# Summing a state scan's sixteen products on TensorE alone, instead of pairing them by accumulating DMAs first

## The chip, the cores and the metric

The kernel runs on one core of a Trainium2 chip. The metric is the device time of one execution in microseconds (us). Three executions of the kernel before took 10943.48, 10928.4 and 10927.6 us: the median is 10928.4 us.

## What is computed

The reference has two layers on a tensor `x` of 16 images, 128 channels, 64 x 64 pixels (4096 tokens an image). Cut to what matters here:

```python
# layer 0: a state space scan over the tokens of each image
xz = gn(x) @ W_in;  xs, z = split(xz)                 # 256 inner channels each
xc = silu(causal_conv(xs, conv_w) + conv_b)           # 4 taps
dt, Bm, Cm = split(xc @ W_xproj, [8, 8 + 16])
delta = softplus(dt @ W_dt + b_dt)
h_new = exp(delta * A) * h + (delta * xc)[:, :, None] * B_t   # 16 states n per channel
y = (h_new * C_t).sum(n) + xc * D
x = x + ((y * silu(z)) @ W_out)
# layer 1: attention with a running maximum and running sums over the tokens, 8 heads
k, v = silu(ln(t) @ W_kv);  s = q . k
m = cummax(s);  e = exp(s - m);  t = t + mean_over_heads(cumsum(e * v) / cumsum(e))
# then a gated feed-forward layer on 8 chosen tokens of each of 64 experts
```

The change is in the sum over `n` (the 16 states), and in the order of some steps of layer 1's attention that run in the same loop.

## The kernel before, in words

**The main loop** (line 710) runs over `k`: 128 blocks of 512 tokens (8 blocks an image), then 10 more rounds. Round `k` does three things at once: the scan of block `k` (`cur`), preparation of block `k + 1` (`nxt`: normalisation, convolution, projections), and the attention of a block nine behind (`m = k - 9`, and `mp_`, the one before it, whose second half is still open). So rounds 0 to 8 have scan alone, rounds 9 to 127 have all, and the last rounds have attention alone. After the loop come a routing stage, the experts, and the final sum (lines 922 to 1183).

**One round is 16 steps** `n`, one for each state (line 880). In step `n`, in this order: `product` (VectorE, `bx = du * B_n`), `beside(n)` (a list, written by hand, of work of the other blocks on TensorE and ScalarE, lines 734 to 878), `decays` (ScalarE, `da = exp(delta * A_n)` for up to eight states ahead), `load_bc` (SyncE's queue loads the rows B and C of three states ahead, broadcast to all partitions), `scan` (two VectorE scans of 128x512 with `between(n)` between them, then GpSimd's product `da <- h * C_n` into the tile of the decay), and `keep_state`. Every engine executes its own instructions in the order in which they are written down here; nothing is moved by a scheduler (`InOrder`, line 23, through which all of them go: hence the profile puts almost everything on L31, and tiles tell the operations apart).

**The sum over the states.** GpSimd leaves 16 tiles `da` of 128 x 2 x 512 a round. In steps 1, 3, ..., 13, `add_pair` (line 375, called at line 894) issues an accumulating DMA from GpSimd's queue that adds tile `n - 1` to tile `n`: 7 DMAs a round of 512 KB each. `add_y` (line 386) then adds one tile to the PSUM tile `y_ps`: 8 TensorE transposes of 128x128 in float32, each with its weight load. It is called for 9 tiles a round: the seven pair sums (at the ends of steps 4, 6, ..., 14 of the same round, line 899, and in step 0 of the next, line 745) and tiles 14 and 15 (step 1 of the next round), and once more for the term `xc * D` (step 2, which begins the sum). `take_y` (ScalarE, step 1), `turn_y` (8 transposes, step 2) and `gate` (VectorE, step 3, which needs TensorE's `yb_ps`) finish the previous block's y, `out_proj` projects it in step 5.

**What stands around it in the lists.** `weights` (two `w_ps` banks, filled by TensorE, read by ScalarE's exponential into `wm`), followed by `attend`, whose first matmuls `ao_ps` need `wm`. Step 7: `score_log`, the split of two numbers into three bf16 parts (`rest` on TensorE subtracts the part already taken, `split` on ScalarE rounds what is left), `conv(nxt, 1)` (the second product of the convolution: four taps, two passes each), `inverse` (four exponentials `e`), `finish`, and `store_parts` (a DMA from ScalarE's queue). `conv_silu` follows, behind a ScalarE table load. In step 10 `spread_parts` issues 16 small loads of those parts from SyncE's queue, and `load_bc` of later steps stands behind them in that queue. Short PSUM tiles of all kinds share 3 banks (`ps`), the tiles `da` have 13 buffers, the tiles B and C five. `from_chunks` (line 499) carries the running maximum and the running sum from one block to the next: line 510 copies two numbers a partition.

Of the kernel before, what the change touches and what calls it, by code (L numbers as in the profile page):

```python
# [39 lines left out]
def conv_attn_hybrid(ctx: ExitStack, tc: tile.TileContext, x, w_in, conv_w, conv_b, w_xproj, w_dt, b_dt,  # L40
# [40 lines left out]
    with ExitStack() as st:  # L81
# [201 lines left out]
            t = t[:, KC - 1 :] if w["i"] == 0 else t  # L283
            ACT.activation(t, t, AF.Identity, bias=gs[:, 4:5], scale=gs[:, 3:4])

        def conv(k, a):

            w = blocks[k]
            pt = w[f"xs{a}"] = bank("xs_ps")
            for t in range(KC):  # L290
                PE.matmul(pt, wc[:, t, bass.ts(a, P)], w["xb"][:, t : t + L], start=(t == 0), stop=(t == KC - 1))

        def conv_silu(k):
# [205 lines left out]
        def from_chunks(m, what, local, first, op0, op1, data):  # L499

            b, i = divmod(m, NBLK)
            last = stp.tile([P, 32], F32, tag=f"last_{what}", name=f"last_{what}")
            DVE.transpose(last, local[:, P - 32 :])
            z = zs[what][m % 2]
            if i == 0:
                DVE.memset(z[:, 0:10:5], first)
            else:
                DVE.tensor_copy(z[:, 0:10:5], gn[b][what][:, 4:14:5])  # L510
            gn[b][what] = z
            for g in range(2):
                DVE.tensor_tensor_scan(z[:, 5 * g + 1 : 5 * g + 5], bc(data[:, 0:1], [P, CB]),
                                       last[:, 5 * g : 5 * g + 4], z[:, 5 * g : 5 * g + 1], op0, op1)
            back = stp.tile([P, 32], F32, tag=f"back_{what}", name=f"back_{what}")
            DVE.transpose(back, z)
            return back[:, 31:32]
# [151 lines left out]


        LAG = NBLK + 1
        LEAD, LEAD_BC = 8, 3
        order = [(k, n) for k in range(NK) for n in range(N)]
        made = 0
# [35 lines left out]
        for k in range(NK + LAG + 1):  # L710
# [23 lines left out]
            def beside(n):  # L734

                if n == 0:
                    if mp_ is not None:
                        attend_before(mp_, 1)
                        add_x(mp_, 0)
                    if m is not None:  # L740
                        key(m, 0), key(m, 1), key(m, 2)
                    if mp_ is not None:
                        finish(mp_, 0)
                    if prev is not None:
                        add_y(prev, N - 3)
                if n == 1:
                    if m is not None:
                        key(m, 3), key(m, 4)
                        score(m, 0)
                    if prev is not None:  # L750
                        add_y(prev, N - 2)
                        add_y(prev, N - 1)
                    if nxt is not None:
                        norm_block(nxt)
                    if cur is not None:
                        skip(cur)
                    if prev is not None:
                        take_y(prev)
                if n == 2:
                    if m is not None:  # L760
                        key(m, 5), key(m, 6), key(m, 7)
                    if prev is not None:
                        turn_y(prev)
                    if cur is not None:
                        add_y(cur, -1)
                if n == 3:
                    if m is not None:
                        score(m, 1)
                    if prev is not None:
                        gate(prev)  # L770
                    if mp_ is not None:
                        for x in range(4, 8):
                            value(mp_, x // 2, x % 2)
                if n == 4:
                    load_exp()
                    if m is not None:
                        score_max(m)
                    if mp_ is not None:
                        weights(mp_, 2)
                    if ends is not None:  # L780
                        gn_end(ends, 1)
                if n == 5:
                    if mp_ is not None:
                        attend(mp_, 2)
                        weights(mp_, 3)
                    if m is not None:
                        score_exp(m)
                    if prev is not None:
                        out_proj(prev)
                    decays(k, n, 2)  # L790
                    if mp_ is not None:
                        carry_on(mp_, 2)
                if n == 6:
                    if mp_ is not None:
                        attend(mp_, 3)
                        attend_before(mp_, 2)
                    if nxt is not None:
                        conv(nxt, 0)
                    decays(k, n, 2)
                    if prev is not None:  # L800
                        put_back(prev)
                    if mp_ is not None:
                        carry_on(mp_, 3)
                    if ends is not None:
                        gn_end(ends, 3)
                if n == 7:
                    if mp_ is not None:
                        attend_before(mp_, 3)
                        add_x(mp_, 1)
                    if m is not None:  # L810
                        score_log(m)
                        rest(m, 1)
                    decays(k, n, 2)
                    if m is not None:
                        split(m, 1)
                    if nxt is not None:
                        conv(nxt, 1)
                    if m is not None:
                        rest(m, 2)
                        inverse(m)  # L820
                    if mp_ is not None:
                        finish(mp_, 1)
                    if m is not None:
                        split(m, 2)
                        store_parts(m)
                    if nxt is not None:
                        conv_silu(nxt)
                    if ends is not None:
                        gn_end(ends, 4)
                if n == 8:  # L830
                    if m is not None:
                        turn_weights(m)
                        value(m, 0, 0)
                    if nxt is not None:
                        xproj(nxt)
                        store_bc(nxt)
                    if m is not None:
                        value(m, 0, 1)
                if n == 9:
                    if mn is not None:  # L840
                        ln_center(mn)
                        ln_square(mn)
                    if cur is not None:
                        gate_silu(cur)
                    if k + 2 < NK:
                        load_block(k + 2, ACT)
                    if m is not None:
                        value(m, 1, 0), value(m, 1, 1)
                if n == 10:
                    if mn is not None:  # L850
                        ln_var(mn)
                    if nxt is not None:
                        delta(nxt)
                    load_exp()
                    if mn is not None:
                        ln_scale(mn)
                if n == 12:
                    if m is not None:
                        weights(m, 0)
                if n == 13:  # L860
                    if m is not None:
                        attend(m, 0)
                        attend_before(m, 0)
                        weights(m, 1)
                    decays(k, n, 2)
                    if m is not None:
                        carry_on(m, 0)
                if n == 14:
                    if mn is not None:
                        ln_apply(mn)  # L870
                    if m is not None:
                        attend(m, 1)
                    decays(k, n, 2)
                    if m is not None:
                        carry_on(m, 1)
                if n == 15:
                    if stat is not None:
                        gn_stats(*stat)

            for n in range(N):  # L880
                if cur is not None:
                    product(cur, n)
# [5 lines left out]
                if cur is not None:  # L888
# [2 lines left out]
                        load_bc(*order[later])  # L891
                    scan(cur, n, between)
                    keep_state(cur, n)
                    if n % 2 and n < N - 2:
                        add_pair(cur, n)
                else:
                    between(n)
                if cur is not None and n >= 4 and n % 2 == 0:
                    add_y(cur, n - 3)

                if 8 <= n <= 11 and i == 0 and prev is not None:
                    store_residual(b - 1, n - 8)
# [307 lines left out]
```

## Time and profile before

| What | Value |
|---|---|
| Median of three executions | 10928.4 us |
| The profiled execution | 10931.22 us |
| Its span, first to last instruction | 10929.5 us |
| Stretch 650 to 9430 us (rounds with scan and attention): busy TensorE, VectorE, ScalarE, GpSimd | 7915.26, 7760.89, 6248.85, 6827.48 us of 8780 |
| TensorE clock granted over the span | 0.890 |
| Tiles `da` added by DMA: issues, data, time of the packets | 896, 469.82 MB, 22.0% of 16 DMA engines |
| Transposes `y_ps<-ident,da` | 9216, 309 ns each as recorded |

The profile comes from one execution. "Busy" counts recorded instructions; TensorE's are pipelined and their ends are modelled, so starts are used below wherever possible. The clock is the share of full speed that the chip granted to TensorE. A wait is named by the instruction that ended it.

### The profile page before, as it was taken

The page shows a single profiled execution, that of the slowest core. Times are in us where ns is not written, and L with a number is a line of the kernel's source. Part 1 is how long each engine was busy: PE and PEld are TensorE (multiplying, and loading weights), DVE is VectorE, ACT ScalarE, POOL GpSimd, SP SyncE. Part 2 cuts the span into 40 slices and gives each one's busy share as a digit, 9 for nine tenths or more (in the row PEclk, how much of TensorE's full clock was granted, in tenths as well). Part 3 has the DMA queues.
Part 4 walks back from the last instruction along what each step waited for, and adds up shares of the span by engine and source line. Part 5 has one row for each costly group of instructions (what it writes and reads, how often), then busy time and mean ns, then how long its engine had stood idle before and what let it go on. Part 6 is the DMA issues. An engine that isn't in the chain of part 4 may idle for free.

```text
span 10929.5 us, 157776 instructions
## 1 busy us (share of the span) xinstructions
PE 9405.6 (86%) x55389; PEld 5549.3 (51%) x55389; DVE 9012.1 (82%) x9987; ACT 7284.5 (67%) x12924; POOL 7530.3 (69%) x4771
## 2 busy tenths in 40 slices
PE   4579998899988989998899999989899899888875
PEld 2345555555555555555555555555555555544752
DVE  8998888888888888888889888888888888820753
ACT  5567776777777777777777777777777777754640
POOL 7887777778777777777777777777777777820000
PEclk7789998999999999899998998999999899999886
DMA  7777767777677777776777777677777777721348
GB/s 191 199 205 182 198 178 199 181 193 184 179 199 181 195 179 195 185 195 181 187 190 184 194 181 200 176 199 180 193 187 176 198 178 192 184 65 34 109 154 343
DMA packets 944361, 1995.67 MB, mean 183 GB/s; under 512 B 103040, under 2 KB 188688, under 8 KB 936400
## 3 DMA queue, kind: packets, MB, share of 16 engines
q1 hardware_dynamic: 732912, 1414.88, 43.6%
q0 software_dynamic: 129024, 469.82, 22.0%
q10 hardware_dynamic: 81632, 100.88, 2.7%
q8 instruction: 439, 7.19, 0.3%
q14 instruction: 354, 2.90, 0.1%
HBM read 1363.98 MB, written 151.52 MB: 139 GB/s over the span
## 4 chain that ended last, share of the span: by engine, by line
PE 61%; ACT 18%; DVE 7%; DMA 7%; issue 5%; SPq 1%; ACTq 1%; POOL 1%; DVEq 0%; POOLq 0%
PE ao_ps L31 10%; PE k_ps L31 8%; PE v_ps L31 7%; PE xs_ps L31 7%; PE y_ps L31 6%; ACT da L31 5%; PE carry_ps L31 4%; PE o_ps L31 4%; DVE h L31 3%; PE s_ps L31 3%; ACT L219 3%; ACT wm L31 2%; PE dt_ps L31 2%; DVE bx L31 2%; PE dbl_ps L31 2%
## 5 line engine op out<-in xcount | busy, mean ns | idle before, releaser
L31 POOL TENSOR_TENSOR da<-h,bct 128x1024 f32<-128x1024 f32 x2048 | 6475.5, 3162 | 1943.1 <-DVE h L31 1521.5
L31 DVE TENSOR_TENSOR_SCAN h<-da,state,bx 128x512 f32<-128x512 f32 x3584 | 4414.6, 1265 | 169.5 <-DVE bx L31 3.4
L31 DVE TENSOR_TENSOR bx<-du,bct 128x1024 f32<-128x1024 f32 x2048 | 2598.3, 1269 | 470.3 <-DMA bct<-bcs 404.1
L31 ACT ACTIVATE da<-delta,a_neg 128x512 f32<-128x512 f32 x4096 | 2629.8, 716 | 89.5 <-DMA da<-da 61.4
L31 PE MATMUL y_ps<-ident,da 128*128 128x128 f32 x9216 | 1428.1, 309 | 279.2 <-DMA da<-da 278.9
L31 PEld LDWEIGHTS y_ps<-ident,da 128*128 128x128 f32 x9216 | 1210.5, 160 | 719.6 <-issue 401.8
L31 PE MATMUL ao_ps<-wm,v 128*128 128x128 f32 x8192 | 1266.4, 318 | 281.5 <-ACT wm L31 276.4
L31 PEld LDWEIGHTS ao_ps<-wm,v 128*128 128x128 f32 x8192 | 1182.1, 226 | 559.8 <-ACT wm L31 401.8
L31 PE MATMUL v_ps<-wv,xn 128*128 128x512 f32 x2048 | 1035.8, 629 | 257.0 <-ACT xc L31 240.9
L31 ACT ACTIVATE v<-v_ps 128x512 f32<-128x512 f32 x1024 | 606.3, 597 | 778.7 <-PE v_ps L31 669.1
L31 ACT ACTIVATE wm<-w_ps 128x512 f32<-128x512 f32 x1024 | 552.1, 590 | 608.7 <-PE w_ps L31 607.3
L31 PE MATMUL k_ps<-xn,wk 128*128 128x512 f32 x2048 | 944.4, 595 | 1.7 <-ACT kt L31 1.7
L31 PE MATMUL xs_ps<-xb,wc 128*128 128x512 f32 x2048 | 925.3, 595 | 1.8 <-issue 1.8
L31 POOL DMA_DIRECT2D da<-da x896 | 787.7, 879 | 163.9 <-POOL state L31 95.1
L31 PEld LDWEIGHTS v_ps<-wv,xn 128*128 128x128 f32 x2048 | 341.9, 192 | 787.5 <-issue 316.1
L31 ACT ACTIVATE kt<-k_ps 128x512 f32<-128x512 f32 x1024 | 587.3, 600 | 190.0 <-PE k_ps L31 166.2
L31 DVE TENSOR_TENSOR_SCAN h<-da,bx 128x512 f32<-128x512 f32 x512 | 599.8, 1206 | 25.5 <-ACT da L31 0.5
L31 PEld LDWEIGHTS xs_ps<-xb,wc 128*128 128x128 f32 x2048 | 372.0, 191 | 397.1 <-issue 382.5
L31 ACT ACT_TABLE_LOAD x395 | 506.8, 1283 | 51.6 <-ACT parts L31 45.9
L31 PEld LDWEIGHTS k_ps<-xn,wk 128*128 128x128 f32 x2048 | 371.6, 191 | 321.0 <-issue 254.7
L31 POOL COPY state<-h 128x2 f32<-128x2 f32 x1792 | 509.0, 284 | 0.0
L31 DVE TENSOR_TENSOR z<-yb_ps,z 128x512 f32<-128x512 f32 x256 | 164.8, 685 | 339.7 <-PE yb_ps L31 339.3
(196 smaller groups left out, 10931.1 us busy)
## 6 DMA issues: line engine op xcount, KB each, us to landing
bct<-bcs SPq DMA_DIRECT2D x2048, 512.0 KB
da<-da POOLq DMA_DIRECT2D x896, 512.0 KB, 8.1
xs<-t_d SPq DMA_DIRECT2D x240, 256.0 KB
xs<-in_x_dram SPq DMA_DIRECT2D x128, 256.0 KB
xt<-in_x_dram SPq DMA_DIRECT2D x64, 512.0 KB
t_d<-xt SPq DMA_DIRECT2D x64, 512.0 KB
t_d<-xs ACTq DMA_DIRECT2D x256, 128.0 KB
t<-t_d SPq DMA_DIRECT2D x128, 256.0 KB
```

What stands on the lines that cost most here:

```text
L31: return lambda *args, **kw: self.tc.keep_in_program_order(f(*args, **kw))
L219: tc.keep_in_program_order(nc.scalar.preload_act_table_set(EXP_LN))
```

## The change

Four edits, made together.

1. `PAIRS = ()`: no state is paired by a DMA any more; `add_pair` is never called. `add_y` is called for all 16 tiles: tile `n - 2` at the end of step `n` (2 to 15), tiles 14 and 15 in steps 0 and 1 of the next round. In step 8 the call stands ahead of `turn_weights` instead of at the end, so that tiles 5 (end of step 7) and 6 (start of step 8) follow one another.
2. The second product of the convolution is cut in two halves of two taps; `rest(m, 2)` stands between them on TensorE instead of behind all four taps.
3. On ScalarE in step 7: `finish(mp_, 1)` moves ahead of the first `split`, the two states of `decays` move from ahead of the first `split` to behind it, and `split(m, 2)` and `store_parts` move ahead of `inverse`.
4. Line 510's copy of two numbers becomes a `tensor_reduce` with a maximum over one element: the same numbers by another VectorE instruction.

```diff
-        def conv(k, a):
+        def conv(k, a, taps=range(KC)):
             w = blocks[k]
-            pt = w[f"xs{a}"] = bank("xs_ps")
-            for t in range(KC):
+            if taps[0] == 0:
+                w[f"xs{a}"] = bank("xs_ps")
+            pt = w[f"xs{a}"]
+            for t in taps:
                 PE.matmul(pt, wc[:, t, bass.ts(a, P)], w["xb"][:, t : t + L], start=(t == 0), stop=(t == KC - 1))
...
-                DVE.tensor_copy(z[:, 0:10:5], gn[b][what][:, 4:14:5])
+                DVE.tensor_reduce(z[:, 0:10:5], gn[b][what][:, 4:14:5].unsqueeze(2), mybir.AxisListType.X, ALU.max)
...
+        PAIRS = ()
...
                     if prev is not None:
-                        add_y(prev, N - 3)
+                        if N - 3 in PAIRS:
+                            add_y(prev, N - 3)
+                        else:
+                            add_y(prev, N - 2)
                 if n == 1:
...
                     if prev is not None:
-                        add_y(prev, N - 2)
+                        if N - 3 in PAIRS:
+                            add_y(prev, N - 2)
                         add_y(prev, N - 1)
...
                     if m is not None:
                         score_log(m)
+                    if mp_ is not None:
+                        finish(mp_, 1)
+                    if m is not None:
                         rest(m, 1)
-                    decays(k, n, 2)
-                    if m is not None:
                         split(m, 1)
                     if nxt is not None:
-                        conv(nxt, 1)
+                        conv(nxt, 1, range(KC // 2))
+                    decays(k, n, 2)
                     if m is not None:
                         rest(m, 2)
-                        inverse(m)
-                    if mp_ is not None:
-                        finish(mp_, 1)
-                    if m is not None:
                         split(m, 2)
                         store_parts(m)
+                        inverse(m)
+                    if nxt is not None:
+                        conv(nxt, 1, range(KC // 2, KC))
                     if nxt is not None:
                         conv_silu(nxt)
...
                 if n == 8:
+                    if cur is not None:
+                        sums_of_y(n)
                     if m is not None:
                         turn_weights(m)
...
+            def sums_of_y(n):
+                if n - 3 in PAIRS:
+                    add_y(cur, n - 3)
+                if n >= 2 and n - 2 not in PAIRS and n - 1 not in PAIRS:
+                    add_y(cur, n - 2)
...
-                    if n % 2 and n < N - 2:
+                    if n in PAIRS:
                         add_pair(cur, n)
...
-                if cur is not None and n >= 4 and n % 2 == 0:
-                    add_y(cur, n - 3)
+                if cur is not None and n != 8:
+                    sums_of_y(n)
```

More of the change, by code (lines that the diff above doesn't have):

```diff
@@ L811, in beside @@
                         score_log(m)
-                        rest(m, 1)
-                    decays(k, n, 2)
-                    if m is not None:
-                        split(m, 1)
-                    if nxt is not None:
-                        conv(nxt, 1)
-                    if m is not None:
-                        rest(m, 2)
-                        inverse(m)
                     if mp_ is not None:
@@ L823, in beside @@
                     if m is not None:
+                        rest(m, 1)
+                        split(m, 1)
+                    if nxt is not None:
+                        conv(nxt, 1, range(KC // 2))
+                    decays(k, n, 2)
+                    if m is not None:
+                        rest(m, 2)
                         split(m, 2)
                         store_parts(m)
+                        inverse(m)
+                    if nxt is not None:
+                        conv(nxt, 1, range(KC // 2, KC))
                     if nxt is not None:
```

## The prediction

> **What bounds the kernel now.** I read in this order: busy time by stage, waits, then one round in TensorE's and ScalarE's order of time. In the stretches below the columns are length, busy TensorE, weight loads, VectorE, ScalarE, GpSimd (with instructions), clock, DMA share, GB/s.
>
> ```profile
> 1500.00:9300.00 7800.00, 7038.96 (x41066) 4085.92 (x41066) 6886.53 (x6837) 5549.75 (x9707) 6052.15 (x3816) 0.91 0.72 188
> ...
> 5074.50:5079.60 5.10, 3.54 (x14) 1.58 (x14) 3.68 (x3) 3.68 (x5) 4.72 (x4) 1.00 0.70 154
> 5079.60:5089.90 10.30, 9.11 (x51) 6.82 (x50) 8.58 (x8) 7.10 (x12) 6.49 (x5) 0.50 1.02 292
> 5089.90:5107.40 17.50, 16.41 (x130) 11.09 (x129) 13.60 (x12) 15.16 (x27) 14.27 (x10) 1.00 0.59 152
> ```
>
> TensorE and VectorE are both near 90% (7039 and 6887 of 7800): shares don't decide. The last lines show TensorE at half clock for 10 us of a round. Who waits for whom decides (us in all, times, longest):
>
> ```profile
> DVE bx L31 <- DMA bct<-bcs: 353.6, 114, 11.1
> DVE z L31 <- PE yb_ps L31: 290.0, 94, 5.3
> PE v_ps L31 <- ACT xc L31: 208.3, 102, 2.3
> PE ao_ps L31 <- ACT wm L31: 208.3, 302, 0.9
> PE dt_ps L31 <- ACT delta L31: 80.1, 103, 0.8
> ```
>
> From 1500 to 9300 us (103 rounds) VectorE waits 3.4 us a round for B rows and 2.8 us for TensorE's `yb_ps`. TensorE waits some 7 us a round, for ScalarE alone; for a tile of GpSimd or VectorE practically never. ScalarE in turn waits for TensorE. So **the round is the loop TensorE-ScalarE-TensorE**, and VectorE is ahead of it with about 6 us to spare. Rounds 0 to 7, without attention, take 64.5 us from gate to gate on VectorE; rounds with attention average 75.85 us (101 rounds). The round from the gate at 5032.4 us, on TensorE:
>
> ```profile
> 5061.57 0.33 PE L31 MATMUL et_ps<-ident,w 128*128 128x128 f32 x1 [0.46 <-ACT parts L31]
> 5064.22 1.13 PE L31 MATMUL v_ps<-wv,xn 128*128 128x512 f32 x2 [2.32 <-ACT xc L31]
> ...
> 5074.46 1.12 PE L31 MATMUL dt_ps<-dbl,wdt 8*128 8x512 f32 x2
> 5076.36 1.12 PE L31 MATMUL dt_ps<-dbl,wdt 8*128 8x512 f32 x2 [0.78 <-ACT delta L31]
> 5077.41 1.09 PE L31 MATMUL y_ps<-ident,da 128*128 128x128 f32 x8
> 5078.43 0.39 PE L31 MATMUL w_ps<-rh,lh 64*128 64x512 bf16 x1
> 5080.25 0.58 PE L31 MATMUL w_ps<-rh,lh 64*128 64x512 bf16 x1 [1.44 <-ACT rstd L31]
> 5080.77 0.64 PE L31 MATMUL w_ps<-maskb,identb 64*64 64x256 bf16 x4
> 5081.34 1.97 PE L31 MATMUL y_ps<-ident,da 128*128 128x128 f32 x8
> 5083.85 3.78 PE L31 MATMUL ao_ps<-wm,v 128*128 128x128 f32 x16 [0.54 <-ACT wm L31]
> ...
> 5098.69 1.04 PE L31 MATMUL y_ps<-ident,da 128*128 128x128 f32 x8
> 5099.56 1.88 PE L31 MATMUL k_ps<-xn,wk 128*128 128x512 f32 x4
> ```
>
> A tile of y (8 transposes) occupies 5099.56 - 5098.69 = 0.87 us at full clock and 1.97 at half. The holes ahead of `et`, `v`, `w` and `ao` are where more of them could lie for nothing.
>
> [...] half-clock stretches are 3.41, 6.83, 10.24 or 13.65 us; in the 101 rounds 2.0 us a round lie between the first `v` and the first `dt`, 6.8 between `dt` and the next `ao`, 4.7 between that `ao` and `yb`. [...] with `y_ps` transposes alone, busy 3.22 of 3.45 us from 246.30, the clock went from 0.50 to 1.00. [...] the copy of two numbers for the maximum takes 709 ns (median), that for the sum 126.
>
> **The change, part by part.** Per round of 75.85 us, with every engine's list read in the built programs' order.
>
> *Removed:* 7 accumulating DMAs, 470 MB and 22% of the DMA engines in all, and their 0.88 us issues on GpSimd (787.7 us in all). GpSimd waits for VectorE and VectorE has 6 us of slack: worth nothing while TensorE binds; if that cover goes, up to the 3.4 us wait for B.
>
> *Added:* 7 tiles of y, 7 x 0.88 = 6.2 us of TensorE at full clock. By stage:
> - `yb` to `o` (steps 2 to 5): two more. Tile 0 stands ahead of `s` and `v`, no hole there: +0.88. Tile 1 stands ahead of `w`; ScalarE's table load (1.28 us) makes `wm` late anyway, and the 0.91 us hole ahead of `ao` covers it: 0.
> - `o` to `rest`: tile 3, ahead of an `ao` that doesn't wait: +0.88.
> - `rest` to `v` (steps 7, 8): tiles 5 and 6 lie in the 2.4 us hole ahead of `et` and `v`: 0. But ScalarE's new order counts. Before, the decays lay in a 2.3 us hole ahead of `split`:
>
> ```profile
> 5052.77 2.56 ACT L31 ACTIVATE da<-delta,a_neg 128x512 f32<-128x512 f32 x4
> 5057.60 0.37 ACT L31 CAST parts<-rest_ps 128x256 bf16<-128x256 f32 x1 [2.27 <-PE rest_ps L31]
> ...
> 5061.14 0.37 ACT L31 CAST parts<-rest_ps 128x256 bf16<-128x256 f32 x1 [1.73 <-PE rest_ps L31]
> ```
>
>   Counted from the end of `add_x`: `finish` 0.20 to 0.57, its DMA issue to 0.97, `split` to 1.3, decays (2.46 to the next start) to 3.7, `split` 4.1, `store_parts` 4.5, four `e` 5.8, table load 7.1, first silu; `v` follows at 7.83 instead of 7.09 (median): +0.74, at best +0.3 if the issues overlap. The parts leave 0.55 us sooner, so SyncE's 16 small loads and the B loads behind them do too; that shortens a wait of VectorE only.
> - `v` to `dt`: tile 5 has left, tile 7 has come: +-0. With the hole filled, the short half-clock stretch there should go: rounds without it take 10.6 us for this stage, with it 11.95, mean 11.43. I take 10.5: -0.9 (bounds -1.4 and -0.4).
> - `dt` to `yb`: 8 tiles instead of 6, +1.76. ScalarE holds the first `ao` until 9.39 us after `dt` even in quiet rounds (mean 9.77), which covers one tile; tile 11 covers the 0.68 us hole ahead of the second `ao` and costs 0.2; 12 and 13 in step 15 are paid back by one fewer each in steps 0 and 1. Then the clock: over the rounds, `ao` to `yb` fits 20.34 us + 0.42 for each us at half clock (22.3 with 4.7). If denser transposes behind `dt` end the half clock earlier in about half the rounds, 4.7 becomes 2.8: -0.8. Together -0.6. Bounds: no half clock at all 9.39 + 20.34 + 0.2 = 29.9 against 32.07, -2.1; half clock kept throughout, tiles 8 and 9 cost 1.3 more than ScalarE covers and 10 to 13 some 1.7: +3.0.
>
> *The reduce:* no row with its shape; `tensor_reduce` of 8 to 1 takes 166 ns, the copies 126 and 709. I take 0.15: -0.55 us of VectorE, +0.03 for the sum. VectorE has slack: 0; without slack 0.5 x 112 = 60 us.
>
> *The halved convolution* adds no instruction and waits for nothing new except `split` (done 0.9 us before): 0, down to 0.1 either way.
>
> Sum: 0.88 + 0.88 + 0.74 - 0.9 - 0.6 = **+1.0 us a round**. It applies to the 117 or so rounds that have scan, preparation and two attention blocks: +117 us. The first rounds are VectorE's (64.5 us, TensorE half idle), the tail has no y: 0. Made against the profiled execution: 10931.2 + 117 = 11048; the median lies 2.8 us lower: **11045 us**. A measurement of this kernel tells about 0.2% (22 us) from no change.
>
> **Rivals.**
> - *The clock pays for the transposes* (0.30): the filled holes keep the half clock away. At its bounds: 0.88 + 0.88 + 0.74 - 1.4 - 2.1 = -1.0, 10811 us, faster. Place: the stages from `v` to `yb`; it decides once these two together fall by more than 2.5 us. For: 13.5 us of half clock a round, and a window of transposes alone brought the clock back. Against: `dt` (8 rows) and its 0.78 us wait stay, as does ScalarE's 9.39 us.
> - *VectorE was the bound* (0.04): with DMAs and copy gone its two waits go, some 5.5 us x 117, 10290. Against: TensorE has no wait for it.
> - *The half clock grows* (0.12): tiles at half clock delay `w`, `wm` and `ao`: 0.88 + 0.88 + 0.74 - 0.4 + 3.0 = +5.1, 11528; half of it 11230.
> - *The terms cancel* (0.07): 10928.
> - That y isn't summed by TensorE alone is excluded: the built program has 17 groups of 8 a round, none of `da<-da`.
>
> **The numbers.** My forecast 0.47, with 11000 to 11180 of its own. Slower 0.47 + 0.12 = 0.59, same 0.07, faster 0.34. The range leaves out VectorE as the bound and the far half of the growing half clock, and reaches to the bounds of the rest: 10800 to 11250.
>
> **What would show it.** `y_ps<-ident,da` x16384, no `da<-da`; gate to gate near 76.9 us. Right: `yb` to `o` and `o` to `xs` each 0.9 longer, `rest` to `v` 0.7 longer, `v` waiting 1.6 instead of 2.4 us, clock 0.92 to 0.93, TensorE above 93% busy, B wait shorter but VectorE's wait for `yb_ps` longer than 2.8 us a round. Wrong: a clock near 1.00 from `dt` to `yb`, or TensorE waiting for tiles of GpSimd.

## The result, and the profile after

The changed kernel takes **10822.49 us** (median of three, 10816.52 to 10835.9) against 10928.4: ratio 0.9901, 95% interval [0.9879, 0.9924]. It is faster by 106 us where 117 us slower was forecast. Its profiled execution has a span of 10820.7 us and a granted clock of 0.948 (0.890 before).

The page of the kernel after, the clock in 40 slices and the group of the transposes (count, busy us and mean ns, idle time before them):

```profile
PEclk7789999999999999999999999999999999999886
...
L31 PE MATMUL y_ps<-ident,da 128*128 128x128 f32 x16384 | 2262.7, 288 | 177.0 <-POOL da L31 176.5
```

The same row of the clock on the page before:

```profile
PEclk7789998999999999899998998999999899999886
```

The transposes are the 16384 foretold, and the group `da<-da` is gone. They take 288 ns each instead of 309, at the same instruction and shape: in both traces one takes 275 ns in the mean at full clock and 424 to 427 at half, and 2051 of 9216 lie wholly at half clock before, 1364 of 16384 after. The clock reads 9 from the fourth slice to the end of the main loop, where the row before has several 8s; in tenths the two rows hardly differ, so the stretches decide.

Stretches of the kernel after (columns as in the prediction): the steady rounds, then one round cut where its clock changes, beginning with the first `dt` and ending with `yb`:

```profile
1500.00:9300.00 7800.00, 7225.16 (x47320) 4514.64 (x47319) 6967.95 (x6911) 5640.02 (x9815) 5665.58 (x3134) 0.98 0.52 141
5036.35:5039.77 3.42, 2.64 (x9) 1.05 (x9) 2.80 (x3) 1.32 (x3) 2.93 (x3) 1.00 0.81 289
5039.77:5043.18 3.41, 3.41 (x20) 2.65 (x18) 0.39 (x1) 3.35 (x5) 1.76 (x2) 0.50 0.87 226
5043.18:5065.98 22.80, 21.20 (x181) 14.98 (x178) 20.67 (x18) 20.10 (x36) 17.07 (x9) 1.00 0.50 136
```

Clock 0.98 instead of 0.91 over the steady rounds, DMA share 0.52 instead of 0.72. The half clock behind `dt` lasts one stretch of 3.41 us where the round shown of before had 10.3. These rounds are typical: from 1500 to 9200 us, the half clock behind `dt` lasts 10.2 us or more in 100 of 101 rounds of the kernel before, and in the kernel after 3.4 us in 60 of 103 rounds, 6.8 in 16 and nothing in 27. TensorE's order of time in the same round shows what lies there:

```profile
5038.25 1.12 PE L31 MATMUL dt_ps<-dbl,wdt 8*128 8x512 f32 x2 [0.78 <-ACT delta L31]
5039.30 3.27 PE L31 MATMUL y_ps<-ident,da 128*128 128x128 f32 x16
5042.51 0.60 PE L31 MATMUL w_ps<-rh,lh 64*128 64x512 bf16 x2
...
5045.74 2.09 PE L31 MATMUL ao_ps<-wm,v 128*128 128x128 f32 x16 [1.22 <-ACT wm L31]
```

The clock still drops after the stretch with `dt` and its wait (TensorE busy 2.64 of 3.42 us). But tiles 8 and 9 now stand without a pause in the slow stretch (busy 3.41 of 3.41), where before one tile, two `w` and a wait of 1.44 us for `rstd` stood; and the next stretch has the full clock. `ao` takes 2.09 us instead of 3.78.

Waits of TensorE and VectorE after, 1500 to 9300 us (us in all, times, longest):

```profile
DVE z L31 <- PE yb_ps L31: 268.1, 104, 5.1
PE v_ps L31 <- ACT xc L31: 175.3, 104, 1.7
PE ao_ps L31 <- ACT wm L31: 152.9, 103, 1.9
DVE xn L31 <- ACT rstd L31: 150.0, 88, 3.6
DVE bx L31 <- DMA bct<-bcs: 108.3, 74, 4.9
```

VectorE's wait for B fell from 353.6 to 108.3 us, and its longest from 11.1 to 4.9; instead it now waits for ScalarE's `rstd` (150.0, before 10.0 in the same stretch). VectorE was given time and hands it back elsewhere: it is not the bound.

By stage, from starts on TensorE, means of some 100 rounds between 1500 and 9200 us; the half clock is the overlap of each stage with the record of the granted clock:

| Stage | before, us | after, us | change | predicted | half clock before, after |
|---|---|---|---|---|---|
| `yb` to `o` | 13.73 | 14.51 | +0.78 | +0.88 | |
| `o` to `rest` | 11.53 | 12.40 | +0.87 | +0.88 | |
| `rest` to `v` | 7.10 | 7.80 | +0.70 | +0.74 | |
| `v` to `dt` | 11.43 | 10.30 | -1.13 | -0.9 | 2.04, 0.00 |
| `dt` to `ao` | 9.77 | 9.43 | -0.34 | -0.6 with the next | 6.83, 2.14 |
| `ao` to `yb` | 22.30 | 20.57 | -1.73 | | 4.70, 0.94 |
| round | 75.85 | 75.02 | -0.83 | +1.0 | 13.6, 3.1 |

117 rounds at -0.83 make -97 of the -106 us. Three of the five terms fit within 0.1 us, and the fourth lies within its bounds. The miss is the last one, `dt` to `yb`: -2.07 instead of -0.6.

### The profile page after: what moved, and what is told of

It reads as the page before. It is cut to its first block, busy times and chain, and to the rows that moved or that the text cites. A ratio compares the mean times of both kernels' runs of the same rounds, so it can differ in the third digit from the quotient of the medians.

```text
span 10820.7 us, 171459 instructions
## 1 busy us (share of the span) xinstructions
PE 9624.7 (89%) x62557; PEld 6064.2 (56%) x62557; DVE 9018.4 (83%) x9987; ACT 7315.9 (68%) x12924; POOL 6979.1 (64%) x3875
## 4 chain that ended last, share of the span: by engine, by line
PE 66%; ACT 23%; DVE 4%; issue 3%; DMA 3%; ACTq 1%; POOL 1%; SPq 0%; DVEq 0%; POOLq 0%
PE y_ps L31 11%; PE ao_ps L31 10%; PE v_ps L31 8%; PE k_ps L31 8%; ACT da L31 8%; PE carry_ps L31 4%; PE o_ps L31 4%; PE xs_ps L31 4%; PE s_ps L31 3%; ACT wm L31 3%; PE dt_ps L31 3%; PE w_ps L31 3%; PE z_ps L31 2%; PE dbl_ps L31 2%; ACT L219 2%
## 5 line engine op out<-in xcount | busy, mean ns | idle before, releaser
L31 POOL TENSOR_TENSOR da<-h,bct 128x1024 f32<-128x1024 f32 x2048 | 6555.4, 3201 | 2564.7 <-DVE h L31 2004.4
L31 PEld LDWEIGHTS y_ps<-ident,da 128*128 128x128 f32 x16384 | 1975.6, 149 | 912.0 <-issue 587.6
L31 PE MATMUL y_ps<-ident,da 128*128 128x128 f32 x16384 | 2262.7, 288 | 177.0 <-POOL da L31 176.5
L31 PE MATMUL ao_ps<-wm,v 128*128 128x128 f32 x8192 | 1085.5, 288 | 213.3 <-ACT wm L31 209.1
L31 PE MATMUL v_ps<-wv,xn 128*128 128x512 f32 x2048 | 1011.8, 617 | 205.9 <-ACT xc L31 198.1
L31 PEld LDWEIGHTS ao_ps<-wm,v 128*128 128x128 f32 x8192 | 1011.5, 199 | 279.0 <-ACT wm L31 277.0
L31 ACT ACTIVATE xs<-ao_ps 128x256 f32<-128x256 f32 x256 | 97.7, 382 | 438.1 <-PE ao_ps L31 438.1
```

Source lines behind the costliest of these rows:

```text
L31: return lambda *args, **kw: self.tc.keep_in_program_order(f(*args, **kw))
```

## The experiments

**The theory** after the result: the half clock pays. Tiles 8 and 9 behind `dt` and 5 to 7 around `v` end it, and what it gives back exceeds the three costs that nothing hides. **The rival:** the removed DMA traffic, which I had put at nothing, is where the gain comes from. No kernel below leaves out part of the computation; `e4` and `e5` add transposes of the identity matrix that nobody reads and that later results overwrite, and `e3`, `e10`, `e13` and `e14` add DMAs into tiles that nobody reads. Times are medians of 4 runs or more; ratios are to the kernel before on the same chip, with 95% intervals.

### One part of the change at a time

`e1_sums_only` is the kernel after with edits 2, 3 and 4 undone; `e2_step7_only` is the kernel before with edits 2 and 3 alone; `e6_copy` is the kernel after with edit 4 undone:

```diff
-                DVE.tensor_reduce(z[:, 0:10:5], gn[b][what][:, 4:14:5].unsqueeze(2), mybir.AxisListType.X, ALU.max)
+                DVE.tensor_copy(z[:, 0:10:5], gn[b][what][:, 4:14:5])
```

> The first edit alone: all 16 tiles of y by TensorE, at the places of the changed kernel, with step 7 (its order and the undivided convolution) and the copy as before. If the half clock is the cause and ScalarE's new order in step 7 costs the 0.7 us a round that the stage from rest to v shows, this is faster than the changed kernel by 117 x 0.7 = 82 us: about 10740 us. If the new order of step 7 is what made the change faster (the parts leave earlier, VectorE waits less for B), it lies above the changed kernel's 10822, towards 10928 or beyond.

Measured 10765.83, ratio 0.9845 [0.9831, 0.986], near the 10740 expected: the sums alone are worth more than the whole change. `rest` to `v` is back at 7.10 us, the round is 74.47.

> The second and third edits alone: the halved convolution and the new order of step 7, with the pairs still added by DMA. If the loop of TensorE and ScalarE binds: +0.7 us a round in the stage from rest to v, 11010 us, half clock 13.5 us a round as before. If the earlier parts and the shorter wait for B are worth something: below 10928.

Measured 11087.21, ratio 1.0135 [1.0118, 1.0152]: slower, and by 77 us more than expected. `rest` to `v` has the +0.70. But `v` to `dt` also rose, 11.43 to 12.43: ScalarE's new order makes `v` wait 3.35 us instead of some 2, and the half clock in that stage is 3.42 us a round instead of 2.04. As I read it, a cost that the stage itself shows drags a second one behind it by the clock; in the whole change, with tiles in that hole, this stage has no half clock (0.00 us).

> The changed kernel with the copy of two numbers back in place of the reduce. VectorE isn't the bound: the copy takes 0.5 us more a round where GpSimd holds it up, and the time stays within 0.2% of the changed kernel's 10822. If VectorE bound the changed kernel: +0.5 us x 117, 10880 us.

Measured 10828.23, ratio 0.9902 [0.9881, 0.9924]: the reduce is worth nothing here, as said. What it shortens shows in the two traces: in the kernel before, 104 of the 112 copies for the maximum start during a GpSimd product `da<-h,bct` and end 0.02 to 0.03 us after it, at 701 to 781 ns; the other 8 take 126 to 129. After, 104 of the 112 reduces start during such a product too, and all take 110 to 117 ns.

### The clock alone, with all DMAs kept

`e4_idle_dt` is the kernel before with eight unread transposes behind `dt`; `e5_idle_both` has sixteen more ahead of `et`:

```diff
             rp = [bank("w_ps") for _ in range(2)]
+            for d in range(idle):
+                PE.transpose(rp[0][:, bass.ts(d % 4, P)], ident, ident)
...
-                        weights(m, 0)
+                        weights(m, 0, 8)
```

```diff
             et = bank("et_ps")
+            for d in range(16):
+                PE.transpose(et[:, bass.ts(d % 4, P)], ident, ident)
```

> The kernel before with 8 transposes more a round whose result is never read, in the hole between dt and w in step 12; nothing is removed. If a denser stretch there ends the half clock earlier: half clock between ao and yb falls from 4.7 us a round to 2 or less, dt to yb from 32.1 to about 30.5 us, and the kernel gets faster with more work, 10740 to 10810 us. If the clock isn't the cause: not below 10928, up to +0.9 us a round, 11030 us.

Measured **10811.53**, ratio 0.9886 [0.9871, 0.9901]. Nothing is removed and eight transposes a round are added, and the kernel is 1.1% faster, just above the upper end of what was expected (10810). One round of it, first TensorE's order of time behind `dt`, then the stretches of its clock:

```profile
5014.45 1.09 PE L31 MATMUL y_ps<-ident,da 128*128 128x128 f32 x8
5015.38 1.04 PE L31 MATMUL w_ps<-ident 128*128 128x128 f32 x8
```

```profile
5011.50:5020.19 8.69, 6.19 (x35) 3.38 (x34) 4.25 (x5) 7.31 (x10) 5.39 (x5) 1.00 0.90 269
5020.19:5027.02 6.83, 6.12 (x38) 5.12 (x38) 6.79 (x7) 3.58 (x7) 4.45 (x2) 0.50 0.84 235
```

Behind `dt` the clock stays full through all of the transposes; it drops later, ahead of `ao`, and for two stretches (6.83 us), not three. The stage means: half clock from `dt` to `ao` 6.83 to 3.74 us, from `ao` to `yb` 4.70 to 1.24; `ao` to `yb` takes 20.75 us instead of 22.30, where the changed kernel has 20.57. The other hole, left as it was, got worse: `v` to `dt` rose from 11.43 to 11.97 us, with 3.45 us at half clock instead of 2.04.

> The kernel before with idle transposes in both holes: 8 a round between dt and w (as in the run with these alone, 10812 us) and 16 ahead of et in step 8, where TensorE waits 2 us for the silu. If the clock is the cause: the half clock between v and dt (3.4 us a round in that run) goes too, v to dt falls from 12.0 to 10.6 us, and the time to about 10650 us (10620 to 10720), though 24 transposes a round are added and none removed. If not: 10812 or above.

Measured **10696.76**, ratio 0.9786 [0.9769, 0.9804]. With the other hole filled the half clock between `v` and `dt` falls to 0.07 us and that stage to 10.89. With all the traffic kept, the clock is enough by itself for a gain of the change's size.

### The same work at another place

`e9_late89` is the kernel after with tiles 8 and 9 moved from behind `dt` to the end of step 14, where TensorE has full clock and no hole:

```diff
             def sums_of_y(n):
+                if n in (10, 11):
+                    return
+                if n == 14:
+                    add_y(cur, 8), add_y(cur, 9)
```

> The changed kernel with tiles 8 and 9 of y moved from behind dt to the end of step 14, behind the second ao: the same number of transposes, all else as it was. Only the stretch behind dt is thinner. If density there is what ends the half clock: the half clock between ao and yb, 0.9 us a round in the changed kernel, is back near 4 and the two tiles, uncovered, add 0.9 to 1.8 us: +2.3 to 3.5 us a round, 11090 to 11230 us. If the clock has nothing to do with it: only the uncovered tiles, at most +1.8 us a round, 11030 or below.

Measured 11252.99, ratio 1.0293 [1.0276, 1.031]: the same instructions, 430 us slower than the kernel after, and 23 us more than the upper end of what was expected. A round of it, behind `dt`:

```profile
5010.07 0.58 PE L31 MATMUL w_ps<-rh,lh 64*128 64x512 bf16 x1 [1.63 <-ACT rstd L31]
...
5011.15 1.97 PE L31 MATMUL y_ps<-ident,da 128*128 128x128 f32 x8
5013.66 3.78 PE L31 MATMUL ao_ps<-wm,v 128*128 128x128 f32 x16 [0.54 <-ACT wm L31]
```

```profile
5008.85:5019.10 10.25, 8.49 (x48) 6.50 (x48) 8.51 (x9) 7.64 (x13) 4.36 (x2) 0.50 0.92 310
```

The picture of before is back: waits where the tiles stood, 10.25 us at half clock, `ao` 3.78 us. Half clock from `ao` to `yb` 5.02 us a round instead of 0.94, and that stage 24.17 us instead of 20.57. Over its rounds the stage fits 21.95 us + 0.44 for each us at half clock, that of the kernel after 20.17 + 0.43: of the 3.6 us the two tiles without cover are 1.8, the clock is the other half.

### The removed traffic

Two first attempts put seven accumulating DMAs of 512 KB a round back beside the sums on TensorE, into one SBUF tile (`e3_dma_kept`, 12 buffers for `da` instead of 13) and into seven tiles in DRAM (`e10_dma_dram`):

```diff
-                    if n in PAIRS:
-                        add_pair(cur, n)
+                    if n % 2 and n < N - 2:
+                        POOL.dma_start(sink, blocks[cur]["da", n], accum_op=ALU.add)
```

> The changed kernel with the removed traffic put back: in steps 1, 3, ..., 13 an accumulating DMA of the same 512 KB adds a tile to one that nobody reads (12 buffers of the tiles da instead of 13 make room for it). y still comes from TensorE alone. If the half clock is the cause: within 0.3% of the changed kernel, 10800 to 10850 us. If less DMA traffic (22% of the engines' time) was the gain: back to about 10928 us, with VectorE's wait for B at 3 us a round again.

> The removed DMAs put back once more, without the flaw of the first attempt (where seven DMAs a round added to one tile and waited for one another, and VectorE's products got slower): 512 KB accumulated from a tile da to one of seven tiles in DRAM that nobody reads, in steps 1, 3, ..., 13, all 13 buffers kept. If DMA traffic wasn't what the change gained from: within 0.3% of the changed kernel, 10790 to 10855 us, with VectorE's wait for B longer and its wait for yb_ps shorter. If it was: near 10910 again.

Both came out as the rival has it: 10910.13, ratio 0.9979 [0.9968, 0.999], and 10940.22, ratio 1.0001 [0.9994, 1.0008], though the half clock stays as rare as in the kernel after (0.98 and 1.00 us from `ao` to `yb`). But neither repeats the traffic of before. With one tile, GpSimd's issue waits 113 times from 1500 to 9300 us until an earlier transfer into it has landed (236.6 us in all, up to 6.0), and the eight first rounds, VectorE's alone, grew from 64.5 to some 68 us. The DRAM tiles add traffic to DRAM that the kernel before didn't have: the queue's packets take 26.2% of the engines (24.8% before, 1500 to 9200 us), and VectorE waits 549 us for B (352 before). How much of their loss these flaws make isn't shown. A cleaner pair: two SBUF tiles in turn, made room for by 11 buffers for `da`, and the same without DMAs as its control.

```diff
-        dap = st.enter_context(tc.tile_pool(name="dap", bufs=13))
+        dap = st.enter_context(tc.tile_pool(name="dap", bufs=11))
...
+                    if n in (1, 3, 5, 7, 9, 11, 13):
+                        POOL.dma_start(sinks[n // 2 % 2], blocks[cur]["da", n], accum_op=ALU.add)
```

> The changed kernel with 11 instead of 13 buffers for the tiles da, as the control of the next two. Without pairs a tile is free once its eight transposes are done, so 11 should be enough: 10822 us within 0.3% (10790 to 10855). If the decays made ahead of time need the other two buffers, ScalarE waits for TensorE's y_ps and the time is above 10855.

Measured 10834.35, ratio 0.9902 [0.9884, 0.9921]: a sound control.

> As e12_bufs11, plus the seven accumulating DMAs of 512 KB a round from the odd tiles da, into two tiles in SBUF that nobody reads, in turn, so that each has two more steps to finish than with one such tile. This is the DMA traffic that the change removed, with the sums still on TensorE. If the clock is the whole gain and the loss in the two earlier runs came from their own flaws (transfers that wait for one another; traffic to HBM), the time is that of e12_bufs11 within 0.3%. If the traffic itself delays the loads of B and the other transfers that the round waits for, the time is 60 to 120 us above e12_bufs11 and VectorE waits 2 us a round or more for B instead of 1.0.

Measured 10879.94, ratio 0.9946 [0.9931, 0.9961]: 46 us above the control, between the two cases of the expectation. The traffic isn't worth nothing. Its DMAs are like those removed, first before, then `e13_sinks7`, 1500 to 9200 us (KB, median us to landing):

```profile
da<-da POOLq DMA_DIRECT2D x711, 512.0 KB, 8.2
```

```profile
sink<-da POOLq DMA_DIRECT2D x714, 512.0 KB, 8.2
```

> As e13_sinks7, with the DMAs of steps 9, 11 and 13 alone. If traffic costs only where it meets the small loads of the parts and the loads of B behind them (steps 9 to 15), this run carries most of the loss of e13_sinks7; if it costs by its amount, three sevenths of it. If traffic costs nothing, the time of e12_bufs11 within 0.3%.

Measured 10829.94, ratio 0.9896 [0.9875, 0.9918]: three of the seven, the late ones, cost nothing. VectorE's waits for B from 1500 to 9200 us, first the control, then `e14_sinks_late`, then `e13_sinks7`:

```profile
DVE bx L31 <- DMA bct<-bcs: 100.1, 72, 4.1
```

```profile
DVE bx L31 <- DMA bct<-bcs: 383.2, 101, 6.2
```

```profile
DVE bx L31 <- DMA bct<-bcs: 420.7, 112, 11.0
```

The sums of the last two hardly differ, and one of them costs 0.4% and the other nothing. What differs is the longest: 11.0 us against 6.2. VectorE has about 6 us to spare (its two waits a round before, 3.4 and 2.8 us), so I read it that waits up to that are absorbed (in `e14_sinks_late` the waits for `yb_ps` and `rstd` shrink in return, from 263.4 and 161.7 us in the control to 208.7 and 8.8), and that what exceeds it lengthens the round. This isn't shown: the rounds of `e3_dma_kept` are 0.4 us longer than those of the kernel after, and its longest wait for B is 5.5 us. By the position of the round in its image of eight, from gate to gate on VectorE, rounds of `e13_sinks7` are longer than the control's mainly at two: 77.12 against 74.88 us at one, 79.16 against 76.98 at the other (the other six average 74.65 against 74.74). Together that is the +0.5 us of the mean. At the first, SyncE's queue also holds an image's four stores (`t_d<-xt`, 512 KB each). The queue of `e13_sinks7` in such a round (start, us of the issue; `lh` and `rh` are the small loads of the parts):

```profile
6634.95 0.37 SPq L31 DMA_DIRECT2D bct<-bcs  x1
6635.37 0.52 SPq L31 DMA_DIRECT2D t_d<-xt  x1
...
6645.35 0.28 SPq L31 DMA_DIRECT2D rh<-pd  x1
6647.71 0.23 SPq L31 DMA_DIRECT2D lh<-pd  x1
...
6652.76 0.39 SPq L31 DMA_DIRECT2D bct<-bcs  x1
```

and VectorE's first product that needed the rows of the last of these lines:

```profile
6658.06 1.23 DVE L31 TENSOR_TENSOR bx<-du,bct 128x1024 f32<-128x1024 f32 x1 [7.98 <-DMA bct<-bcs]
```

Between two loads of B lie 17.8 us. At this position the longest gap averages 17.9 us here, 17.6 in the kernel before, 13.1 in the control and 13.3 in the kernel after. But the round that follows gives most of the delay back: 72.76 us against 74.30. At the second position VectorE waits up to 4.4 us for ScalarE's `gs` in the kernel after, the control and `e13_sinks7` (2.4 in the kernel before); why traffic costs 2.2 us more there I have not traced. The kernel before, with its own traffic, has 76.37 us at that position, less than the kernel after (76.90). So what the traffic costs in this setting is measured, and how it costs it stays open.

### Fewer costs, same clock

`e7_pairs3` is the kernel after with `PAIRS = (1, 3, 5)`: the pairs 0+1, 2+3 and 4+5 go by DMA again, which empties the two places where a tile lay in the open. `e8_pairs3_old7` undoes edits 2 and 3 as well. `e11_pairs4` adds a fourth pair to that:

```diff
-        PAIRS = (1, 3, 5)
+        PAIRS = (1, 3, 5, 13)
```

> The changed kernel with three of the seven pairs (0 and 1, 2 and 3, 4 and 5) added by DMA again; the tiles in the holes behind dt and ahead of et stay on TensorE. Tiles 0 and 3, which lie on TensorE's path at 0.87 us each by the stages, leave it: -1.7 us a round, 10620 us (10580 to 10680). If every pair put back brings back cost (DMA traffic, VectorE's wait for B): 10822 or above.

> As the run with three pairs, and with step 7 in the order of before (undivided convolution): 0.5 to 0.7 us a round less on ScalarE's path, 10540 us (10500 to 10600), if VectorE, busy 69 us a round, doesn't bind first; if it does, near 10620 with its waits for yb_ps near zero.

Measured 10632.83, ratio 0.9728 [0.971, 0.9745], and **10520.4**, ratio 0.9625 [0.961, 0.964]: the fastest here, 3.7% below the kernel before. In `e8` all three unhidden costs are gone (`yb` to `o` 13.64, `o` to `rest` 11.53, `rest` to `v` 7.10) and the clock remains good (3.6 us at half a round).

> As the run with three pairs and the old step 7 (10520 us), with the pair 12 and 13 by DMA too: one tile less on TensorE's path between the second ao and yb, -0.9 us a round, 10420 us, if TensorE and ScalarE still bind. VectorE waits only 1.5 us a round for yb_ps there; if its own work and its wait for B begin to bind, 10450 to 10510.

Measured 10739.29, ratio 0.982 [0.9805, 0.9834]: a miss, 219 us slower than `e8`. Its waits, 1500 to 9200 us, and below them the one of `e8` to compare:

```profile
DVE z L31 <- PE yb_ps L31: 327.9, 104, 8.2
...
PE carry_ps L31 <- ACT carry L31: 181.3, 104, 5.1
ACT da L31 <- DMA da<-da: 129.1, 79, 4.6
```

```profile
PE carry_ps L31 <- ACT carry L31: 39.9, 106, 0.4
```

ScalarE, whose instructions stay in order, stands up to 4.6 us in front of a decay whose tile a DMA still holds, a wait that `e8` doesn't have; `carry` and thus TensorE's `carry_ps` queue behind it. The new hole costs by the clock too: half clock from `ao` to `yb` rises from 0.58 us a round in `e8` to 2.32, and that stage from 20.42 to 22.10 us. I had costed the pair at TensorE and at the clock, and not at the tile.

## Why the prediction was wrong

- **The bound, and the three costs in the open: right.** +0.88, +0.88 and +0.74 were foretold, +0.78, +0.87 and +0.70 came. Tiles 1, 5 and 6 cost nothing where a hole was named for them. `v` waits 1.7 us (1.6 foretold).
- **`v` to `dt`: right**, -1.13 against -0.9 in bounds -1.4 and -0.4; with the traffic put back (`e13`) it is 10.57 us, -0.86.
- **The failed step: "If denser transposes behind `dt` end the half clock earlier in about half the rounds, 4.7 becomes 2.8: -0.8. Together -0.6."** They end it in most rounds: in 83 of 103, no half clock is left between `ao` and `yb`; the mean is 0.94 us and not 2.8, and `dt` to `yb` fell by 2.07 us, to the lower bound of -2.1. `e4` shows that transposes behind `dt` do this with everything else as before, and `e9` that the kernel loses it without them. The mechanism had been named and its size guessed. The trace of before held the better guess: its 163 half-clock stretches between 1500 and 9200 us last one to five times 3.41 us (60 of them 3.41, 64 10.24, 34 13.65), full clock followed the one stretch of transposes alone (busy 3.22 of 3.45 us), and two tiles at half clock (twice 1.97 us from the row shown) are longer than 3.41. If two tiles behind `dt` do what that stretch did, the half clock was to end early in most rounds, not in half of them; that is an estimate from these numbers, and one stretch doesn't show it. The kernel after agrees: in the round shown, the stretch at half clock, most of it transposes, is busy for 3.41 of 3.41 us, and the full clock follows.
- **"Worth nothing while TensorE binds": wrong by 0.5 us a round.** `e13` against its control gives 46 us. I had set VectorE's mean wait of 3.4 us against its slack of 6; the row of the waits had 11.1 us as its longest, which may be the reason. Even with this term at nothing the sign was wrong: `e13` has the traffic back and is still 0.5% faster than before. By this pair some 46 of the 106 us are the traffic's and some 60 the clock's, net of three costs worth about 2.4 us a round. That split holds for this imitation of the traffic; the two flawed ones lose 0.8% and 1.0% against the kernel after, where this one loses 0.4%.
- **The signs to look for:** VectorE's wait for `yb_ps` should have grown beyond 2.8 us a round and is 2.6; the clock is 0.948 instead of 0.92 to 0.93. Both belong to the failed step. TensorE is busy 92.6% of the steady rounds (over 93% foretold).
- **The rival "the clock pays for the transposes"** (0.30, 10811 us, from 2.5 us on) was the right one: the two stages fell together by 3.20 us. Evidence for it stood in the prediction (a window of transposes alone had brought the clock back); I let the waits that stay count against it more than that reading. (The list of half-clock lengths left out three of 17.1 us among 163; nothing rests on them.)

## What to carry to other kernels

In this kernel a hole in TensorE's list costs its wait and, if the clock drops, part of what follows (`e9` against the kernel after: 4.1 us a round more at half clock between `ao` and `yb`, by the fit 1.8 us of time): read the clock beside the order of time, and try filling the hole, or the stretch behind the drop, with useful transposes, or even useless ones. Work added there can be free or better (`e4`: eight transposes a round more, 1.1% faster), the same work at another place can cost (`e9`: two tiles a round moved, 430 us slower): place each part by the hole it lies in. Look at the longest wait that an engine's slack must absorb, and not at the mean alone (here a reading that isn't shown). Let DMAs carry early what would lie in the open (`e7`, three pairs: ratio 0.9728 where all tiles on TensorE have 0.9901), as long as the tile they hold isn't the next that an in-order engine needs (`e11`, a fourth pair: 219 us slower than `e8`).

## What the runs showed of the hardware

- Unread float32 transposes of 128x128 made the kernel faster twice: 8 a round 10811.53 us, ratio 0.9886 (`e4`), 24 a round 10696.76 us, 0.9786 (`e5`). The half clock from `v` to `yb` fell from 13.6 us a round to 8.4 in `e4`.
- A stretch with `dt` and its wait, recorded busy for 2.64 of 3.42 us, was followed by half clock in the kernel after. What part `dt` (8 rows) or `w` (64 rows, bf16) has in such a drop isn't shown.
- Fitted over the rounds of each of the sixteen kernels here, a us at half clock between `ao` and `yb` goes with 0.42 to 0.49 us of time.
- An accumulating DMA of 512 KB between SBUF tiles lands 8.2 us (median) after its issue in `e13`; three a round beside the loads of B (`e14`) raised VectorE's wait for them from 1.0 to 3.7 us a round and the time by nothing (10829.94 us, control 10834.35); with seven (`e13`) the longest wait was 11.0 us and the time 0.4% more (10879.94).
